# A mixture-of-experts block on one core: logits and shared first product merged, shared second products on two row tiles, later loads behind the first weights

## The chip, the cores and the metric

The kernel runs on one core of one Trainium2 chip. The time is the device time of one execution in microseconds; less is better.

## The reference

The input has 8 samples of 512 tokens of 128 numbers, all float32. Three sublayers follow each other, each on a layer norm of the running value x: a mixture-of-experts block (added at half weight), a gated mixing block, and the same mixture-of-experts block again with the same weights.

```python
# the experts, on xf of 512 tokens x 128 per sample
shared = silu(xf @ Ws_up) @ Ws_down                 # 128 -> 64 -> 128
aff = xf @ centroids.T                              # logits of 64 experts
idx = top_k(aff + expert_biases, 8)
w = sigmoid(aff[idx]); w = w / (sum(w) + 1e-8)      # cw: weights, 0 elsewhere
h = silu(einsum('td,edf->etf', xf, W_up))           # all 64 experts, 128 -> 64
y = einsum('etf,efd->etd', h, W_down)               # 64 -> 128
out = shared + einsum('etd,te->td', y, cw)

# the mixing block
xf = concat([u[:, :1], u[:, 1:] @ WB.T]);  xb = concat([u[:, 1:] @ WBf.T, u[:, -1:]])
gamma = sigmoid(xf @ w1.T + xb @ w2.T + b)
y = gamma * (xf + xb) + (1 - gamma) * u
```

In xf the first token of a sample is taken over unmultiplied, in xb the last one.

## The kernel before

The work is cut into 16 items: sample s in layer 0 for s = 0 to 7, then the same samples in layer 1. An item has its 512 tokens in the free dimension. `ut` is its normed input turned to [128 numbers, 512 tokens].

Two experts make a pair, so that a pair's hidden rows fill 128 partitions; an item has 32 pairs. With the shared expert as block 0 it has 33 blocks, and one loop over n = 0, 1, ... runs through the blocks of all items. In step n the order of the work is written out by hand:

- `up(n)`, L376: one product of the pair's first weights with `ut` into `ph` (four PSUM buffers), and a Silu on ScalarE into `h` (L385, L387). For block 0 the weights are `wsup`, with 64 columns.
- `scale(n - 16)`, L390: VectorE multiplies `h` by the experts' weights `cw`, which lie on the 64 partitions of each expert (L397). Block 0 is not scaled. A group of `cw` holds four pairs, and four such buffers exist; when a group is used up, `load_cw` (L288) issues the load of the group four further on, as two transfers of 512 KB that spread a row to 64 partitions.
- `down(n - 19)`, L403: one product of `h` with the pair's second weights, summed in `y` over the 33 blocks (L410). For block 0 the weights are `wsdn`, with 64 rows. After an item's last block ScalarE halves `y` into `yt`, and two steps later `finish` (L360) turns it back into `po` and VectorE adds it to x.
- one slice of `prep(i + 1)`, L301, a generator that prepares the next item and starts in its predecessor's block 1 (for the first item in block `SCALE_LAG - 2` = 14): for layer 1 first `mix`; then the norm, the turn into `ut` (L313), the logits `pa` (four products with 64 columns, L318), the choice of eight experts on VectorE with a Sigmoid on ScalarE (L327, with a change of function table there and back), and the turn of the weights into `pc` (four transposes, L353), copied to `cw_sb` and written to `cw_t` in HBM (L357), from where `load_cw` spreads them.

In `mix`, the two results of a tile of tokens are summed in PSUM as `pfb` by a product with `mix_b` (L236) and one with `mix_bf` (L244); for the first and last tile a third product with the matrices `first` and `last` (L233, L252) puts in the token that is not multiplied. `make_mix` prepares the mix weights, in slices during item 1.

All loads are issued on one queue, SP, in the order of the program: x of sample 0, `cent`, `wsup`, the first weights `wup` in four transfers (one eighth, one eighth, one quarter and one half of them), `wsdn`, the second weights `wdn` in four transfers with x of sample 1 between, the other samples (L97), and the mix weights (L137 to L144). What `prep` and `load_cw` issue for the first item stands behind all these on the queue.

Of the kernel before, what the change touches and what calls it, by code (L numbers as in the profile page):

```python
# [8 lines left out]
F32 = mybir.dt.float32  # L9
AF = mybir.ActivationFunctionType  # L10
ALU = mybir.AluOpType
AX = mybir.AxisListType

P = 128
# [1 line left out]
EPS_W = 1e-8  # L16
LOWEST = -3.4028234663852886e38
GROUP = 4
SCALE_LAG = 16
DOWN_LAG = 19  # L20
CW_BUFS = 4


@with_exitstack
def macaron_kernel(
# [27 lines left out]

    nc = tc.nc
    B, T, D = x.shape
    E, _, F = w_up.shape
    NT = T // P
    NP = E // 2  # L60
    NG = NP // GROUP
    D1 = D + 1
    assert D == P and 2 * F == P and NP % GROUP == 0

    const = ctx.enter_context(tc.tile_pool(name="const", bufs=1))
    resid = ctx.enter_context(tc.tile_pool(name="resid", bufs=1))
# [16 lines left out]
    make_identity(nc, ident)  # L83
    minus_half = const.tile([P, NT], F32, name="minus_half")
    nc.gpsimd.memset(minus_half, -0.5)

    first = const.tile([P, P], F32, name="first")
    last = const.tile([P, P], F32, name="last")
    nc.gpsimd.memset(first, 0.0)
    nc.gpsimd.memset(last, 0.0)  # L90
    nc.gpsimd.tensor_copy(first[:, 0:1], ident[:, 0:1])
    nc.gpsimd.tensor_copy(last[:, P - 1 : P], ident[:, P - 1 : P])
    warm = const.tile([P, 1], F32, name="warm")
    nc.scalar.activation(warm, ident[:, 0:1], AF.Silu)

    def load_x(s):
        nc.sync.dma_start(out=xs[s], in_=x[s].rearrange("(n p) d -> p n d", p=P))  # L97

    wup = const.tile([P, E, F], F32, name="wup")
    wdn = const.tile([P, NP, D], F32, name="wdn")  # L100
    wsup = const.tile([P, F], F32, name="wsup")
    wsdn = const.tile([F, D], F32, name="wsdn")
    cent = const.tile([E, D], F32, name="cent")
    bias_bc = const.tile([P, E], F32, name="bias_bc")
    wb_sb = const.tile([D, D], F32, name="wb_sb")
# [10 lines left out]
    def load_down(e0, e1):  # L116
        nc.sync.dma_start(  # L117
            out=wdn[:, e0 // 2 : e1 // 2, :],
            in_=w_down[e0:e1].rearrange("(q two) f d -> (two f) q d", two=2),
        )  # L120

    load_x(0)
    nc.sync.dma_start(out=cent, in_=centroids)
    nc.sync.dma_start(out=wsup, in_=ws_up)
    load_up(0, E // 8)
    nc.sync.dma_start(out=bias_bc, in_=expert_biases.partition_broadcast(P))
    load_up(E // 8, E // 4)
    load_up(E // 4, E // 2)
    load_up(E // 2, E)
    nc.sync.dma_start(out=wsdn, in_=ws_down)  # L130
    load_down(0, E // 4)
    load_x(1)
    for e0 in range(E // 4, E, E // 4):
        load_down(e0, e0 + E // 4)
    for s in range(2, B):
        load_x(s)
    nc.sync.dma_start(out=wb_sb, in_=wb)  # L137
    nc.sync.dma_start(out=wbf_sb, in_=wbf)
    nc.sync.dma_start(out=w12[:, 0, :], in_=w1[0].partition_broadcast(P))
    nc.sync.dma_start(out=w12[:, 1, :], in_=w2[0].partition_broadcast(P))  # L140
    with nc.allow_non_contiguous_dma(reason="two columns, once"):
        nc.sync.dma_start(out=w12c[:, 0:1], in_=w1.rearrange("o d -> d o"))
        nc.sync.dma_start(out=w12c[:, 1:2], in_=w2.rearrange("o d -> d o"))
    nc.sync.dma_start(out=b_bc, in_=b.partition_broadcast(P))  # L144

    def transposed(dst, src, rows):
        ps = ps_m.tile([P, 512], F32, tag="m", name="turn_ps")
        nc.tensor.transpose(ps[:, :rows], src, ident[:rows, :rows])
        nc.scalar.copy(dst, ps[:, :rows])

    cent_t = const.tile([P, E], F32, name="cent_t")
    transposed(cent_t, cent, E)

    mix_b = const.tile([P, D1], F32, name="mix_b")
    mix_bf = const.tile([P, D1], F32, name="mix_bf")
# [47 lines left out]
    def mix(s):  # L203
# [22 lines left out]
        for half in range(NT // 2):  # L226
            pfb = ps_m.tile([P, 2, D1], F32, tag="m", name=f"pfb{s}_{half}")
            halves.append(pfb)
            for k in range(2):
                j = 2 * half + k  # L230
                edge = j == 0
                if edge:
                    nc.tensor.matmul(  # L233
                        pfb[:, k, :], lhsT=first, rhs=u[:, j, :], start=True, stop=False
                    )
                nc.tensor.matmul(  # L236
                    pfb[:, k, :],
                    lhsT=ut[:, j * P : (j + 1) * P],
                    rhs=mix_b,
                    start=not edge,  # L240
                    stop=False,
                )
                edge = j == NT - 1
                nc.tensor.matmul(  # L244
                    pfb[:, k, :],
                    lhsT=ut[:, j * P + 1 : (j + 1) * P + 1],
                    rhs=mix_bf,
                    start=False,
                    stop=not edge,
                )  # L250
                if edge:
                    nc.tensor.matmul(  # L252
                        pfb[:, k, :], lhsT=last, rhs=u[:, j, :], start=False, stop=True
                    )
            nc.scalar.activation(  # L255
                gam[:, 2 * half : 2 * half + 2],
                pfb[:, :, D],
                AF.Tanh,
                bias=half_b,
                scale=0.5,  # L260
            )
            yield
# [19 lines left out]

    items = [(layer, s) for layer in range(2) for s in range(B)]
    uts = {}
    cw_ts = {}
    cw_tiles = {}

# [13 lines left out]
    def prep(i):  # L301

        layer, s = items[i]
# [9 lines left out]
        nc.scalar.copy(ut, ps)  # L313
        uts[i] = ut
        yield
        pa = ps_m.tile([P, NT, E], F32, tag="m", name=f"pa{i}")
        for j in range(NT):
            nc.tensor.matmul(  # L318
                pa[:, j, :], lhsT=ut[:, j * P : (j + 1) * P], rhs=cent_t, start=True, stop=True
            )  # L320
        yield
        biased = route.tile([P, NT, E], F32, tag="biased", name=f"biased{i}")
# [25 lines left out]
        )  # L348
        yield
        yield  # L350
        pc = ps_m.tile([P, 512], F32, tag="m", name=f"pc{i}")
        for j in range(NT):
            nc.tensor.transpose(pc[:E, j * P : (j + 1) * P], cw[:, j, :], ident)  # L353
        cw_sb = route.tile([E, T], F32, tag="cw_sb", name=f"cw_sb{i}")
        nc.scalar.copy(cw_sb, pc[:E, :])  # L355
        cw_t = dram.tile([E, T], F32, tag="cw_t", name=f"cw_t{i}")
        nc.sync.dma_start(out=cw_t, in_=cw_sb)  # L357
        cw_ts[i] = cw_t

    def finish(i, yt):  # L360
# [7 lines left out]
            nc.sync.dma_start(out=out[s].rearrange("(n p) d -> p n d", p=P), in_=xs[s])  # L368


    NB = NP + 1
    hs = {}
    ys = {}
    later = {}

    def up(n):  # L376
        i, blk = divmod(n, NB)
        rows = F if blk == 0 else P
        ph = ps_up.tile([P, T], F32, tag="ph", name=f"ph{n}")
        if blk == 0:  # L380
            w = wsup
        else:
            pair = blk - 1
            w = wup[:, 2 * pair : 2 * pair + 2, :].rearrange("d e f -> d (e f)")
        nc.tensor.matmul(ph[:rows, :], lhsT=w, rhs=uts[i], start=True, stop=True)  # L385
        h = hid.tile([P, T], F32, tag="h", name=f"h{n}")
        nc.scalar.activation(h[:rows, :], ph[:rows, :], AF.Silu)  # L387
        hs[n] = h

    def scale(n):  # L390
        i, blk = divmod(n, NB)
        if blk == 0:
            return
        q, g = divmod(blk - 1, GROUP)
        group = i * NG + q
        h = hs[n]
        nc.vector.tensor_tensor(h, h, cw_tiles[group][:, g, :], ALU.mult)  # L397
        if g == GROUP - 1:
            cw_tiles.pop(group)
            if group + CW_BUFS < len(items) * NG:  # L400
                load_cw(group + CW_BUFS)

    def down(n):  # L403
        i, blk = divmod(n, NB)
        if blk == 0:
            ys[i] = ps_y.tile([P, T], F32, tag="y", name=f"y{i}")
            w, h = wsdn, hs.pop(n)[:F, :]
        else:
            w, h = wdn[:, blk - 1, :], hs.pop(n)
        nc.tensor.matmul(ys[i], lhsT=w, rhs=h, start=blk == 0, stop=blk == NB - 1)  # L410
        if blk == NB - 1:
            yt = norm.tile([P, T], F32, tag="yt", name=f"yt{i}")
            nc.scalar.mul(yt, ys.pop(i), 0.5)  # L413
            later[n + 2] = lambda: finish(i, yt)

    total = len(items) * NB
    coming = prep(0)
    while 0 not in uts:
        next(coming)
    mixing = make_mix()  # L420
    for n in range(total + DOWN_LAG):
        i, blk = divmod(n, NB)
        if n < total:
            if blk == 0 and i > 0:
                for _ in coming or ():
                    pass
            if i > 0 and blk == 1 or i == 0 and blk == SCALE_LAG - 2:
                for _ in coming or ():
                    pass
                if i == 0:  # L430
                    for g in range(CW_BUFS):
                        load_cw(g)
                coming = prep(i + 1) if i + 1 < len(items) else None
            up(n)
        if 0 <= n - SCALE_LAG < total:
            scale(n - SCALE_LAG)
        if n >= DOWN_LAG:
            down(n - DOWN_LAG)
        if n - DOWN_LAG in later:
            later.pop(n - DOWN_LAG)()  # L440
        if coming is not None and n < total:
            next(coming, None)
        if i == 1 and n < total:
            next(mixing, None)
    for k in sorted(later):
        later[k]()
# [40 lines left out]
```

## Time and profile before

| what | value |
|---|---|
| median of 3 runs | 1003.58 us (1003.48 to 1003.65) |
| profiled execution, its own time | 1002.36 us |
| span of the profiled execution | 1000.6 us |
| mean granted clock of TensorE | 0.996 |
| TensorE busy | 982.5 us, 98% of the span |
| VectorE, ScalarE, GpSimd busy | 457.8, 399.7, 40.0 us |
| HBM traffic | 145 GB/s over the span |

TensorE is written PE, VectorE DVE, ScalarE ACT, GpSimd POOL, the load queue SP or SPq. A float32 product appears as two records, one for each of two passes, and a float32 transpose as one. Matmuls are pipelined and the ends of their records are modelled, so records of neighbours overlap: what a product costs is read from the distance between starts.

### The profile page before, as it was taken

What the parts mean: (1) busy time and instruction counts of PE and PEld (TensorE: products, weight loads), DVE (VectorE), ACT (ScalarE), POOL (GpSimd) and SP (SyncE); (2) the same over time, 40 slices, a digit from 0 to 9 for tenths busy, and PEclk for the clock granted to TensorE, in tenths of its full rate; (3) what the DMA queues carried; (4) which work ended last, traced back from release to release, by engine and by line L of the source; (5) the groups of instructions that cost most, each with busy time, mean ns of one, the idle gap of its engine ahead of it and who ended that gap; (6) DMA issues with size and microseconds to landing.
All of it is one profiled execution on the core that took longest, in us unless ns stands there. A gap on an engine that the chain in (4) does not pass through costs nothing.

```text
span 1000.6 us, 8408 instructions
## 1 busy us (share of the span) xinstructions
PE 982.5 (98%) x2631; PEld 451.6 (45%) x2631; DVE 457.8 (46%) x1232; ACT 399.7 (40%) x656; POOL 40.0 (4%) x75
## 2 busy tenths in 40 slices
PE   7799999999999999999999999999999999999997
PEld 3344444444444444454444544445444454444443
DVE  3344544234453324636256362563626637166051
ACT  4434343443434334334343343433434334343330
POOL 1000000000000000000000000000000000000000
PEclk9899999999999999999999999999999999999999
DMA  9899757578665678737749377593775937659751
GB/s 230 181 215 202 145 113 148 117 163 169 142 140 119 145 138 174 162 85 156 150 106 193 83 168 144 112 201 84 167 142 117 203 80 170 134 120 206 153 125 23
DMA packets 90206, 145.67 MB, mean 146 GB/s; under 512 B 9648, under 2 KB 23600, under 8 KB 90160
## 3 DMA queue, kind: packets, MB, share of 16 engines
q1 hardware_dynamic: 90160, 145.12, 69.4%
q8 instruction: 21, 0.34, 0.2%
q14 instruction: 25, 0.20, 0.1%
HBM read 140.90 MB, written 4.19 MB: 145 GB/s over the span
## 4 chain that ended last, share of the span: by engine, by line
PE 95%; SPq 2%; DMA 2%; DVE 0%; issue 0%; ACT 0%; DVEq 0%
PE y L410 46%; PE ph L385 44%; PE pa L318 1%; PE po L365 1%; PE pfb L244 1%; PE pfb L236 1%; DMA cw<-cw_t 1%; PE pc L353 1%; SPq L97 1%; PE ps_ft L200 1%; DMA x<-in_L_attn_u_dram 1%; SPq L112 0%; SPq L117 0%; SPq L130 0%; DMA cw_t<-cw_sb 0%; PE ps_mixt L200 0%
## 5 line engine op out<-in xcount | busy, mean ns | idle before, releaser
L410 PE MATMUL y<-h,wdn 128*128 128x512 f32 x1024 | 522.4, 595 | 6.0 <-DVE h L397 6.0
L385 PE MATMUL ph<-ut,wup 128*128 128x512 f32 x1024 | 525.9, 598 | 0.0
L387 ACT ACTIVATE h<-ph 128x512 f32<-128x512 f32 (+1 forms) x528 | 313.2, 597 | 508.1 <-PE ph L385 475.7
L397 DVE TENSOR_TENSOR h<-h,cw 128x512 f32<-128x512 f32 x512 | 319.0, 682 | 40.4 <-DMA cw<-cw_t 35.0
L410 PEld LDWEIGHTS y<-h,wdn 128*128 128x128 f32 x1024 | 193.5, 190 | 256.5 <-issue 214.1
L385 PEld LDWEIGHTS ph<-ut,wup 128*128 128x128 f32 x1024 | 188.1, 191 | 213.0 <-issue 201.1
L366 DVE TENSOR_TENSOR x<-po,x 128x512 f32<-128x512 f32 x16 | 11.1, 692 | 171.2 <-PE po L365 171.2
L264 DVE TENSOR_SCALAR sg<-gam 128x4 f32<-128x4 f32 x8 | 1.4, 170 | 162.1 <-ACT gam L255 162.1
L323 DVE TENSOR_TENSOR biased<-pa,bias_bc 128x256 f32<-128x256 f32 x16 | 6.8, 424 | 122.0 <-PE pa L318 122.0
L179 POOL TENSOR_SCALAR rstd_f<-mv_f 128x4 f32<-128x4 f32 x16 | 8.5, 532 | 585.8 <-DVE mv_f L177 585.8
L186 DVE TENSOR_SCALAR u_f<-x,mv_f,rstd_f 128x128 f32<-128x128 f32 x64 | 17.8, 342 | 20.4 <-POOL rstd_f L180 20.4
L318 PEld LDWEIGHTS pa<-cent_t,ut 128*128 128x128 f32 x128 | 17.5, 200 | 9.0 <-issue 8.3
L327 ACT ACT_TABLE_LOAD x16 | 20.5, 1283 | 0.3
L387 ACT ACT_TABLE_LOAD x16 | 20.5, 1283 | 0.3
L385 PE MATMUL ph<-ut,wsup 128*64 128x512 f32 x32 | 18.1, 647 | 0.7 <-ACT ut L313 0.7
L410 PE MATMUL y<-h,wsdn 64*128 64x512 f32 x32 | 18.0, 641 | 0.0
L413 ACT ACTIVATE yt<-y 128x512 f32<-128x512 f32 x16 | 9.6, 597 | 20.5 <-PE y L410 20.5
L318 PE MATMUL pa<-cent_t,ut 128*128 128x64 f32 x128 | 17.1, 279 | 0.0
L180 POOL TENSOR_TENSOR rstd_f<-rstd_f,minus_half 128x4 f32<-128x4 f32 x16 | 16.6, 1038 | 1.3
L175 DVE BATCH_NORM_STATS2 st_f<-x 128x6 f32<-128x128 f32 x64 | 13.8, 276 | 3.5 <-DMA x<-in_L_attn_u_dram 3.5
L355 ACT COPY cw_sb<-pc 64x512 f32<-64x512 f32 x16 | 9.3, 580 | 14.0 <-PE pc L353 12.9
L179 POOL TENSOR_SCALAR rstd_mix<-mv_mix 128x4 f32<-128x4 f32 x8 | 4.6, 577 | 253.6 <-DVE mv_mix L177 253.6
(72 smaller groups left out, 280.0 us busy)
## 6 DMA issues: line engine op xcount, KB each, us to landing
cw<-cw_t SPq DMA_DIRECT2D x256, 512.0 KB, 8.2
x<-in_L_attn_u_dram SPq DMA_DIRECT2D x8, 256.0 KB, 5.5
wdn<-in_L_ffn_W_down_dram SPq DMA_DIRECT2D x4, 512.0 KB, 6.5
cw_t<-cw_sb SPq DMA_DIRECT2D x16, 128.0 KB, 3.3
out_dram<-x SPq DMA_DIRECT2D x8, 256.0 KB, 2.8
wup<-in_L_ffn_W_up_dram SPq DMA_DIRECT2D x2, 256.0 KB, 3.7
wup<-in_L_ffn_W_up_dram SPq DMA_DIRECT2D x1, 512.0 KB, 6.2
w<-in_L_attn_w_dram SPq DMA_DIRECT2D x2, 64.0 KB, 4.8
```

Of the source, the lines that this page charges most:

```text
L97: nc.sync.dma_start(out=xs[s], in_=x[s].rearrange("(n p) d -> p n d", p=P))
L175: nc.vector.bn_stats(st[:, j, :], src[:, j, :])
L179: nc.gpsimd.tensor_scalar(rstd, mv[:, :, 1], EPS_LN, None, ALU.add)
L180: nc.gpsimd.tensor_tensor(rstd, rstd, minus_half, ALU.pow)
L186: nc.vector.tensor_scalar(u[:, j, :D], src[:, j, :], mv[:, j, 0:1], rstd[:, j : j + 1], ALU.subtract, ALU.mult,)
L318: nc.tensor.matmul(pa[:, j, :], lhsT=ut[:, j * P : (j + 1) * P], rhs=cent_t, start=True, stop=True)
L327: nc.scalar.activation(sig, pa, AF.Sigmoid)
L366: nc.vector.tensor_tensor(xs[s], po, xs[s], ALU.add)
L385: nc.tensor.matmul(ph[:rows, :], lhsT=w, rhs=uts[i], start=True, stop=True)
L387: nc.scalar.activation(h[:rows, :], ph[:rows, :], AF.Silu)
L397: nc.vector.tensor_tensor(h, h, cw_tiles[group][:, g, :], ALU.mult)
L410: nc.tensor.matmul(ys[i], lhsT=w, rhs=h, start=blk == 0, stop=blk == NB - 1)
```

## The change

- One tile `wsl` [128, 2, 2, 64] holds the logits' and the shared expert's first weights twice, in both orders. For each half of the tokens one product `sl` of 128 columns gives both: for the first half the shared rows on partitions 0 to 63 and the logits on 64 to 127, for the second half the other way round. VectorE copies the logits to `lg`, ScalarE applies Silu to the shared rows into `hsh`, both [128, 256]: the two halves of the tokens on the two halves of the partitions. Block 0 is gone; an item has 32 steps.
- The logits are turned by two 128 x 128 transposes into `pa`. The weights `cw` are turned by two transposes into `pc` [128, 256], in place of four, and written by two transfers.
- The shared second product is made for half of the tokens at a time with 64 rows of `wsdn`, which lies on both halves of the partitions. During an even item i, after the downs of pairs 8 and 16, two such products follow each other: one for item i on one half of the partitions, one for item i + 1 on the other, each into its own item's `y`.
- In `mix` the products with `first` and `last` are gone; VectorE adds the token to `pfb` ahead of tanh. The two matrices and their four GpSimd operations go.
- On the SP queue x of sample 1 stands ahead of `wdn`, of which half follows in two transfers; the rest (`wsdn` twice, the other half of `wdn`, the samples from 2 on, the mix weights) is issued after the first four groups of `cw`.
- `SCALE_LAG` is 22 and `DOWN_LAG` 25; `h` has 28 buffers for 22. `prep(1)` starts in pair 14 of item 0, and `make_mix` runs during item 2.

The diff, cut:

```diff
-SCALE_LAG = 16
-DOWN_LAG = 19
+SCALE_LAG = 22
+DOWN_LAG = 25
 CW_BUFS = 4
+FIRST = 14
+SHARED = (8, 16)
...
-    wsup = const.tile([P, F], F32, name="wsup")
-    wsdn = const.tile([F, D], F32, name="wsdn")
+    wsl = const.tile([P, 2, 2, F], F32, name="wsl")
+    wsdn = const.tile([P, D], F32, name="wsdn")
...
-    nc.sync.dma_start(out=wsup, in_=ws_up)
+    for k in range(2):
+        nc.sync.dma_start(out=wsl[:, k, k, :], in_=ws_up)
     load_up(0, E // 8)
...
-    nc.sync.dma_start(out=wsdn, in_=ws_down)
+    load_x(1)
     load_down(0, E // 4)
-    load_x(1)
-    for e0 in range(E // 4, E, E // 4):
-        load_down(e0, e0 + E // 4)
...
+    load_down(E // 4, E // 2)
+
+    def load_rest():
+        for k in range(2):
+            nc.sync.dma_start(out=wsdn[k * F : (k + 1) * F, :], in_=ws_down)
+        load_down(E // 2, E)
+        for s in range(2, B):
+            load_x(s)
+        nc.sync.dma_start(out=wb_sb, in_=wb)
...
+    for k in range(2):
+        nc.scalar.copy(wsl[:, k, 1 - k, :], turn_ps[:, :E])
...
-                if edge:
-                    nc.tensor.matmul(
-                        pfb[:, k, :], lhsT=last, rhs=u[:, j, :], start=False, stop=True
-                    )
+            k, j, at = ((0, 0, 0), (1, NT - 1, P - 1))[half]
+            nc.vector.scalar_tensor_tensor(
+                pfb[:, k, :], u[:, j, :], ident[:, at : at + 1], pfb[:, k, :], ALU.mult, ALU.add
+            )
...
+        for k in range(2):
+            nc.tensor.matmul(
+                sl[:, k, :],
+                lhsT=wsl[:, k, :, :].rearrange("d a f -> d (a f)"),
+                rhs=ut[:, k * H : (k + 1) * H],
+                start=True,
+                stop=True,
+            )
+            at, other = slice(k * F, (k + 1) * F), slice((1 - k) * F, (2 - k) * F)
+            nc.vector.tensor_copy(lg[other, :], sl[other, k, :])
+            nc.scalar.activation(hsh[at, :], sl[at, k, :], AF.Silu)
+        shared[i] = hsh
+        yield
         pa = ps_m.tile([P, NT, E], F32, tag="m", name=f"pa{i}")
-        for j in range(NT):
-            nc.tensor.matmul(
-                pa[:, j, :], lhsT=ut[:, j * P : (j + 1) * P], rhs=cent_t, start=True, stop=True
+        for j in range(NH):
+            nc.tensor.transpose(
+                pa[:, 2 * j : 2 * j + 2, :].rearrange("p c e -> p (c e)"),
+                lg[:, j * P : (j + 1) * P],
+                ident,
             )
...
-        for j in range(NT):
-            nc.tensor.transpose(pc[:E, j * P : (j + 1) * P], cw[:, j, :], ident)
...
+        for j in range(NH):
+            nc.tensor.transpose(
+                pc[:, j * P : (j + 1) * P],
+                cw[:, 2 * j : 2 * j + 2, :].rearrange("p c e -> p (c e)"),
+                ident,
+            )
...
-        nc.sync.dma_start(out=cw_t, in_=cw_sb)
+        nc.sync.dma_start(out=cw_t[:, H:], in_=cw_sb[:E, :])
+        nc.sync.dma_start(out=cw_t[:, :H], in_=cw_sb[E:, :])
...
+        if i % 2 == 0 and pair in SHARED:
+            if i + 1 not in ys:
+                ys[i + 1] = ps_y.tile([P, T], F32, tag="y", name=f"y{i + 1}")
+            k = SHARED.index(pair)
+            for at, item in sorted(((k, i), (1 - k, i + 1))):
+                rows = slice(at * F, (at + 1) * F)
+                nc.tensor.matmul(
+                    ys[item][:, at * H : (at + 1) * H],
+                    lhsT=wsdn[rows, :],
+                    rhs=shared[item][rows, :],
+                    start=item > i and k == 0,
+                    stop=False,
+                )
...
                 if i == 0:
                     for g in range(CW_BUFS):
                         load_cw(g)
+                    load_rest()
```

More of the change, by code (lines that the diff above doesn't have):

```diff
@@ L62, in macaron_kernel @@
     D1 = D + 1
-    assert D == P and 2 * F == P and NP % GROUP == 0
+    H = T // 2
+    NH = NT // 2
+    assert D == P and 2 * F == P and E == F and NT == 4 and NP % GROUP == 0
     const = ctx.enter_context(tc.tile_pool(name="const", bufs=1))
@@ L85, in macaron_kernel @@
     nc.gpsimd.memset(minus_half, -0.5)
[L87 to L92, printed above, removed]
     warm = const.tile([P, 1], F32, name="warm")
@@ L129, in macaron_kernel @@
     load_up(E // 2, E)
-    nc.sync.dma_start(out=wsdn, in_=ws_down)
+    load_x(1)
     load_down(0, E // 4)
-    load_x(1)
-    for e0 in range(E // 4, E, E // 4):
-        load_down(e0, e0 + E // 4)
[L135 to L144, printed above, removed]
+    load_down(E // 4, E // 2)
[6 more added lines that the diff above has]
+        nc.sync.dma_start(out=wb_sb, in_=wb)
+        nc.sync.dma_start(out=wbf_sb, in_=wbf)
+        nc.sync.dma_start(out=w12[:, 0, :], in_=w1[0].partition_broadcast(P))
+        nc.sync.dma_start(out=w12[:, 1, :], in_=w2[0].partition_broadcast(P))
+        with nc.allow_non_contiguous_dma(reason="two columns, once"):
+            nc.sync.dma_start(out=w12c[:, 0:1], in_=w1.rearrange("o d -> d o"))
+            nc.sync.dma_start(out=w12c[:, 1:2], in_=w2.rearrange("o d -> d o"))
+        nc.sync.dma_start(out=b_bc, in_=b.partition_broadcast(P))
     def transposed(dst, src, rows):
@@ L149, in transposed @@
         nc.scalar.copy(dst, ps[:, :rows])
-    cent_t = const.tile([P, E], F32, name="cent_t")
-    transposed(cent_t, cent, E)
+    turn_ps = ps_m.tile([P, 512], F32, tag="m", name="cent_ps")
+    nc.tensor.transpose(turn_ps[:, :E], cent, ident[:E, :E])
+    for k in range(2):
+        nc.scalar.copy(wsl[:, k, 1 - k, :], turn_ps[:, :E])
     mix_b = const.tile([P, D1], F32, name="mix_b")
@@ L230, in mix @@
                 j = 2 * half + k
-                edge = j == 0
-                if edge:
-                    nc.tensor.matmul(
-                        pfb[:, k, :], lhsT=first, rhs=u[:, j, :], start=True, stop=False
-                    )
                 nc.tensor.matmul(
@@ L239, in mix @@
                     rhs=mix_b,
-                    start=not edge,
+                    start=True,
                     stop=False,
                 )
-                edge = j == NT - 1
                 nc.tensor.matmul(
@@ L248, in mix @@
                     start=False,
-                    stop=not edge,
+                    stop=True,
                 )
-                if edge:
-                    nc.tensor.matmul(
-                        pfb[:, k, :], lhsT=last, rhs=u[:, j, :], start=False, stop=True
-                    )
+            k, j, at = ((0, 0, 0), (1, NT - 1, P - 1))[half]
+            nc.vector.scalar_tensor_tensor(
+                pfb[:, k, :], u[:, j, :], ident[:, at : at + 1], pfb[:, k, :], ALU.mult, ALU.add
+            )
             nc.scalar.activation(
@@ L284, in macaron_kernel @@
     uts = {}
+    shared = {}
     cw_ts = {}
@@ L315, in prep @@
         yield
-        pa = ps_m.tile([P, NT, E], F32, tag="m", name=f"pa{i}")
-        for j in range(NT):
-            nc.tensor.matmul(
-                pa[:, j, :], lhsT=ut[:, j * P : (j + 1) * P], rhs=cent_t, start=True, stop=True
+        sl = ps_m.tile([P, 2, H], F32, tag="m", name=f"sl{i}")
+        hsh = small.tile([P, H], F32, tag="hsh", name=f"hsh{i}")
+        lg = route.tile([P, H], F32, tag="lg", name=f"lg{i}")
+        for k in range(2):
[3 more added lines that the diff above has]
+                rhs=ut[:, k * H : (k + 1) * H],
+                start=True,
+                stop=True,
+            )
[4 more added lines that the diff above has]
+        yield
+        pa = ps_m.tile([P, NT, E], F32, tag="m", name=f"pa{i}")
+        for j in range(NH):
[3 more added lines that the diff above has]
+                ident,
             )
@@ L350, in prep @@
         yield
-        pc = ps_m.tile([P, 512], F32, tag="m", name=f"pc{i}")
-        for j in range(NT):
-            nc.tensor.transpose(pc[:E, j * P : (j + 1) * P], cw[:, j, :], ident)
-        cw_sb = route.tile([E, T], F32, tag="cw_sb", name=f"cw_sb{i}")
-        nc.scalar.copy(cw_sb, pc[:E, :])
+        pc = ps_m.tile([P, H], F32, tag="m", name=f"pc{i}")
+        for j in range(NH):
[4 more added lines that the diff above has]
+            )
+        cw_sb = route.tile([P, H], F32, tag="cw_sb", name=f"cw_sb{i}")
+        nc.scalar.copy(cw_sb, pc)
         cw_t = dram.tile([E, T], F32, tag="cw_t", name=f"cw_t{i}")
-        nc.sync.dma_start(out=cw_t, in_=cw_sb)
+        nc.sync.dma_start(out=cw_t[:, H:], in_=cw_sb[:E, :])
+        nc.sync.dma_start(out=cw_t[:, :H], in_=cw_sb[E:, :])
         cw_ts[i] = cw_t
@@ L368, in finish @@
             nc.sync.dma_start(out=out[s].rearrange("(n p) d -> p n d", p=P), in_=xs[s])
-    NB = NP + 1
     hs = {}
@@ L376, in up @@
     def up(n):
-        i, blk = divmod(n, NB)
-        rows = F if blk == 0 else P
+        i, pair = divmod(n, NP)
         ph = ps_up.tile([P, T], F32, tag="ph", name=f"ph{n}")
[L380 to L385, printed above, removed]
+        w = wup[:, 2 * pair : 2 * pair + 2, :].rearrange("d e f -> d (e f)")
+        nc.tensor.matmul(ph, lhsT=w, rhs=uts[i], start=True, stop=True)
         h = hid.tile([P, T], F32, tag="h", name=f"h{n}")
-        nc.scalar.activation(h[:rows, :], ph[:rows, :], AF.Silu)
+        nc.scalar.activation(h, ph, AF.Silu)
         hs[n] = h
     def scale(n):
[L391 to L395, printed above, removed]
+        group, g = divmod(n, GROUP)
         h = hs[n]
@@ L403, in down @@
     def down(n):
-        i, blk = divmod(n, NB)
-        if blk == 0:
+        i, pair = divmod(n, NP)
+        if pair == 0 and i not in ys:
             ys[i] = ps_y.tile([P, T], F32, tag="y", name=f"y{i}")
[L407 to L411, printed above, removed]
+        nc.tensor.matmul(
+            ys[i],
+            lhsT=wdn[:, pair, :],
+            rhs=hs.pop(n),
+            start=pair == 0 and i % 2 == 0,
+            stop=pair == NP - 1,
+        )
[5 more added lines that the diff above has]
+                rows = slice(at * F, (at + 1) * F)
+                nc.tensor.matmul(
+                    ys[item][:, at * H : (at + 1) * H],
[3 more added lines that the diff above has]
+                    stop=False,
+                )
+        if pair == NP - 1:
             yt = norm.tile([P, T], F32, tag="yt", name=f"yt{i}")
@@ L414, in down @@
             later[n + 2] = lambda: finish(i, yt)
-    total = len(items) * NB
+    total = len(items) * NP
     coming = prep(0)
-    while 0 not in uts:
+    while 0 not in shared:
         next(coming)
@@ L421, in macaron_kernel @@
     for n in range(total + DOWN_LAG):
-        i, blk = divmod(n, NB)
+        i, pair = divmod(n, NP)
         if n < total:
-            if blk == 0 and i > 0:
+            if pair == 0 and i > 0:
                 for _ in coming or ():
                     pass
-            if i > 0 and blk == 1 or i == 0 and blk == SCALE_LAG - 2:
+            if i > 0 and pair == 1 or i == 0 and pair == FIRST:
                 for _ in coming or ():
@@ L442, in macaron_kernel @@
             next(coming, None)
-        if i == 1 and n < total:
+        if i == 2 and n < total:
             next(mixing, None)
```

## The prediction

> **What bounds the kernel now.** I read the head of the page and its chain first, then TensorE's groups by form, then TensorE's timeline around each odd matmul, then the start with all engines. From the page:
>
> ```profile
> span 1000.6 us, 8408 instructions
> ...
> PE 982.5 (98%) x2631; PEld 451.6 (45%) x2631; DVE 457.8 (46%) x1232; ACT 399.7 (40%) x656; POOL 40.0 (4%) x75
> ...
> PE 95%; SPq 2%; DMA 2%; DVE 0%; issue 0%; ACT 0%; DVEq 0%
> ```
>
> TensorE holds 95% of the chain and no other engine is half busy. What leaves TensorE shortens the run; what moves among the others does not, unless it makes TensorE wait. The groups by form (the columns are busy, mean ns of one record; a product has two) give the candidates:
>
> ```profile
> L385 PE MATMUL ph<-ut,wsup 128*64 128x512 f32 x32 | 18.1, 647 | 0.7 <-ACT ut L313 0.7
> L410 PE MATMUL y<-h,wsdn 64*128 64x512 f32 x32 | 18.0, 641 | 0.0
> L318 PE MATMUL pa<-cent_t,ut 128*128 128x64 f32 x128 | 17.1, 279 | 0.0
> L353 PE MATMUL pc<-ident,cwtok 128*64 128x128 f32 x64 | 9.6, 273 | 0.0
> L252 PE MATMUL pfb<-u_mix,last 128*128 128x129 f32 x16 | 3.1, 274 | 0.0
> ```
>
> These means include pipeline time that overlaps the next record, so I price by distance between starts. TensorE's timeline (start, length, operation):
>
> ```profile
> 302.29 1.02 PE L410 MATMUL y<-h,wdn 128*128 128x512 f32 x2
> 303.24 1.07 PE L385 MATMUL ph<-ut,wsup 128*64 128x512 f32 x2
> 304.24 1.12 PE L410 MATMUL y<-h,wdn 128*128 128x512 f32 x2
> 305.20 1.02 PE L385 MATMUL ph<-ut,wup 128*128 128x512 f32 x2
> ...
> 337.88 1.02 PE L385 MATMUL ph<-ut,wup 128*128 128x512 f32 x2
> 338.83 1.12 PE L410 MATMUL y<-h,wsdn 64*128 64x512 f32 x2
> 339.88 1.12 PE L385 MATMUL ph<-ut,wup 128*128 128x512 f32 x2
> 340.84 1.02 PE L410 MATMUL y<-h,wdn 128*128 128x512 f32 x2
> ```
>
> Ordinary products start 0.859 us apart (two passes of 0.43). Three products around wsup take 2.91 us, so wsup costs 2.91 - 2 x 0.859 = 1.19; wsdn likewise 2.96 - 1.72 = 1.24. A half-array product thus costs 0.33 to 0.38 more than a full one. The same subtraction at 313.37 to 315.98 prices the four logits products at 0.89 (eight passes of 0.107). The four pc transposes take 0.44, 0.11 each, as do the 128 x 128 ones of ps_ft and po. Products of 129 columns stand 0.22 apart.
>
> The start, all engines (start, length, queue or engine):
>
> ```profile
> 20.20 0.59 ACT L355 COPY cw_sb<-pc 64x512 f32<-64x512 f32 x1
> ...
> 28.51 0.49 SPq L357 DMA_DIRECT2D cw_t<-cw_sb  x1
> ...
> 32.15 18.67 SPq L296 DMA_DIRECT2D cw<-cw_t  x12
> ...
> 39.95 1.90 DVE L397 TENSOR_TENSOR h<-h,cw 128x512 f32<-128x512 f32 x3 [18.02 <-DMA cw<-cw_t]
> 40.69 2.07 PE L410 MATMUL y<-h,wdn 128*128 128x512 f32 x2 [5.95 <-DVE h L397]
> ```
>
> The first weights cw are ready at 20.8 but written at 28.5, since SP first issues every load down to b_bc (27.6). That ends in TensorE's only long wait, 5.95. It costs more: the granted clock is 0.68 from 41 to 45 us, and down, up to the next down take 3.22 instead of 1.72. So 6.1 (34.6, where that down would have started, to 40.69) + 1.5 = 7.6 us.
>
> **What the Trainium skill says.** "TensorEngine Tiling (Array Packing)", Key Properties: changing the tiling mode drains TensorE, changing the tile does not. The trace agrees on the first: a bubble of about 0.2 into wsdn's mode and 0.19 out. No trace of before shows the second. "TensorE: Matmul & The Clock Gate", Part 3: products on different row groups run side by side, but start and end in program order; four tiles gained 3.07 there. Not shown before. Same page, HAM oscillation: idle gaps above about 3.4 us halve the clock; the stall above agrees. "PSUM — Partial Sum Buffer", bank collisions: two row tiles must not write one bank together. Here the two products of a group go to the y of two items, two banks.
>
> **The change, part by part** (16 items).
>
> Removed per item: wsup 1.19, wsdn 1.24, logits 0.89, pc 0.44: 3.77.
>
> Added per item: the product sl, 2 x 256 columns on the full array, no mode change. A pass should take half of 0.43 plus little, 0.216, longer than the 0.107 a weight load needs (the logits' rate). Four passes: 0.87. Then two pa and two pc transposes at 0.11: 0.44.
>
> The shared second products: one group of two 64-row, 256-column products per item on average. Bubbles 0.39 in all, plus four passes of 0.216. If the second product overlaps only the first one's second pass (order kept), three slots: 0.65 + 0.39 = **1.04**, my value. Bounds: wholly side by side 0.43 + 0.39 = 0.82; one after the other 1.25; that with another bubble between, 1.45.
>
> Sum per item: 0.87 + 0.44 + 1.04 - 3.77 = -1.42, times 16 = **-22.7** (-26.2 to -16.2).
>
> Mix: L233 and L252 go, two products of 0.22 in each of 8 items: **-3.5**. In their place VectorE gets two scalar_tensor_tensor (0.34 each, as L268) ahead of tanh. VectorE is 46% busy and downs trail scales by three steps of 1.72, 5.2 us: no cost unless VectorE is already that late. Dropping first and last takes four operations from POOL, idle there anyway.
>
> New work elsewhere: per item two VectorE copies lg (0.42 at most, as biased, also 128x256) and two Silus of 64x256 (about 0.38, as rsig) for one of 0.59; the cw_sb copy halves to about 0.38. They hide beside TensorE. One wait is new: pa now needs lg from VectorE, where before it needed only ut from ScalarE. Between sl and pa stand one up and one down, 1.72 us, against about 0.2 + 2 x 0.42: 0.7 spare. Each hsh Silu waits for its lg copy, and the ups' Silus queue behind; four ph buffers (6.9 us) cover that in the steady state.
>
> SP: one more wsup load (0.57) moves the first up load from 2.45 to 3.0; it lands within about 4 us, before its product at 10. The cw_t write becomes two issues per item, SP being mostly free later.
>
> The start: cw_sb is ready at about 20.5 and the SP queue is empty, so the writes issue at 20.5 and 21, land about 3.4 later, and cw loads begin at 24.5. The first group lands 7.8 later (as 32.15 to 39.95), at 32.3. TensorE reaches the first scale (step 22) at 35 and the first down (step 25) near 38. The stall goes: **-7.6**.
>
> What is late next there: ScalarE. Around steps 18 to 21 it has four Silus, ut, two hsh, sigmoid and two table loads of 1.28, about 7.0 us, while TensorE issues only ups, 0.86 apart, into four buffers. By my walk the Silu of up 21 ends at 37.9, and up 25, which needs its buffer, would start at 36.9: **+1.1** (0 to 2). The table loads fell into the long stall before.
>
> The loads moved behind cw (wsdn twice, half of wdn, x2 to x7, mix weights, 2.9 MB) stand on SP ahead of group 4. Four groups are 4.2 MB, which land at about 215 GB/s (the rate from 36 us on), done at 46; the moved loads at 290 (the rate of 16.5 to 25 us) end near 56; group 4 lands near 63. Its scale is due at step 38, 61.7, its down at 67. VectorE waits, TensorE does not. x2 lands near 51, its statistics are due at 52.
>
> The longer lags move downs from the loop to the tail, each 0.86 in either place: no cost. Scales there need 0.68 against 0.86.
>
> Against wall price, the cold clock until about 16.5 lets slightly less through at the start: +0.2.
>
> Sum: -22.7 - 3.5 - 7.6 + 1.1 + 0.2 = **-32.5**. Against the profiled execution's own 1002.36 (span 1000.6 and 1.8 around it): 969.9. The median shown is 1.2 above that execution: 1003.6 - 32.5 = **971.1 us**.
>
> **The rivals.**
> A. The row tiles don't overlap: +0.21 to +0.41 per item, 974.5 to 977.7. For it: wsdn's 0.38 of bubbles; the passes of one product come first. Against: the page's rule on tiles. Chance 0.22. The opposite, wholly side by side: 967.6, 0.1.
> B. The start's stall moves. If group 4 lands after 67, TensorE waits again; 5 us and 1.5 of cold clock give 977.6. For: SP is in order, 2.9 MB stand ahead. Against: 4 us spare. Chance 0.13.
> C. Slower: pa's new wait on lg. VectorE works in order; a scale waiting for cw (35.0 us in 10 waits in before, 11.7 in 6 between 45 and 965) delays lg, and TensorE, with pa next in order, stalls with no three-step lag. It needs over 32.5 / 16 = 2.0 us at each item, so VectorE 2.7 late every time; at 2.5 a stall the time is 1011. Before's longest wait in that stretch is 3.0, but few. Chance 0.03.
> D. The operations don't leave TensorE (a compiled sl or transpose costs what it replaces): within 2 us of before, 0.01.
> The forecast, 968 to 974, has the remaining 0.51.
>
> **How the numbers follow.** About 0.2%, 2 us, is what the measurement can tell from no change. All cases but C and D are faster: 0.96; same 0.01; slower 0.03. The range 963.5 to 980 takes in the side-by-side case, A and B; A with B (about 984) and C lie outside.
>
> **What would show it.** After: PE busy near 955 of a span near 968; sl passes 0.22 apart; pa and pc two records each of 0.11; from the down before a shared group to the down after it about 1.04 more than without it; no wait of y on h at 35 to 41, a wait of ph on ScalarE's h of about 1 us there; cw_t issued near 20.5. I am wrong on tiles if the groups cost 1.25 or more, on the start if SP or cw still carries a wait of several us, and altogether if TensorE shows waits in every item.

## The result, and the profile after

The changed kernel takes 985.5 us (four runs, 985.12 to 985.68) against 1003.5: a ratio of 0.982 (95% interval 0.9803 to 0.9837). It is shorter by 18.0 us or 1.8%, far outside the spread of the runs, where 32.5 us were forecast; it lies 14.4 above the forecast and 5.5 above the range. The profiled execution took 985.12 us (span 983.0).

Head and chain of the page of the changed kernel:

```profile
span 983.0 us, 8249 instructions
...
PE 954.5 (97%) x2535; PEld 440.8 (45%) x2535; DVE 476.2 (48%) x1280; ACT 398.8 (41%) x673; POOL 39.5 (4%) x71
...
PE 96%; ACT 1%; DVE 1%; DMA 0%; issue 0%; POOL 0%; ACTq 0%
```

TensorE's busy time is 954.5, as forecast (955); the span is not (983 for 968). That the busy time fits is partly luck: the records of sl take 22.0 us here and 17.6 in the first experiment, where the new waits are gone and the busy time is 950.8. Time appeared in which TensorE stands still: 28.5 us outside its busy time, where before had 18.1. The waits of TensorE show for what (line, what it waited for: us in total, times, longest):

```profile
PE sl L327 <- ACT hsh L336: 14.9, 16, 0.9
PE cent_ps L159 <- DMA cent<-in_L_ffn_centroids_dram: 4.0, 1, 4.0
PE ps_ft L209 <- DVE u_f L195: 2.4, 1, 2.4
PE ph L410 <- ACT h L412: 1.7, 2, 0.9
```

Sixteen waits, one per item, each of the same length: a wait built into the code, not a late transfer. The prediction had named waits in every item as the sign that it is wrong altogether. The wait of y on h of before (6.0) is gone, and the one of ph on ScalarE that was expected in its place is there, 0.86 long at 39.98 us. A second one of 0.86 stands at 19.48, in the first item, where none was forecast. TensorE's groups by form (busy, mean ns of one record, idle time before them and what ended it):

```profile
L327 PE MATMUL sl<-ut,wsl 128*128 128x256 f32 x64 | 22.0, 426 | 15.5 <-ACT hsh L336 14.9 <-ACT ut L318 0.7
...
L443 PE MATMUL y<-hsh,wsdn 64*128 64x256 f32 x64 | 11.2, 428 | 0.0
...
L342 PE MATMUL pa<-ident,lg 128*128 128x128 f32 x32 | 6.4, 282 | 0.0
L379 PE MATMUL pc<-ident,cwtok 128*128 128x128 f32 x32 | 6.1, 273 | 0.0
```

One item in the timeline of the changed kernel (start, length, engine, operation, idle time before it and its releaser):

```profile
620.35 1.02 PE L428 MATMUL y<-h,wdn 128*128 128x512 f32 x2
...
621.20 0.59 PE L327 MATMUL sl<-ut,wsl 128*128 128x256 f32 x2
621.84 0.43 DVE L335 COPY lg<-sl 64x256 f32<-64x256 f32 x1 [2.60 <-PE sl L327]
622.30 0.38 ACT L336 ACTIVATE hsh<-sl 64x256 f32<-64x256 f32 x1 [1.16 <-DVE lg L335]
622.73 0.70 PE L327 MATMUL sl<-ut,wsl 128*128 128x256 f32 x2 [0.93 <-ACT hsh L336]
623.26 1.02 PE L410 MATMUL ph<-ut,wup 128*128 128x512 f32 x2
...
624.12 1.02 PE L428 MATMUL y<-h,wdn 128*128 128x512 f32 x2
624.98 0.38 PE L342 MATMUL pa<-ident,lg 128*128 128x128 f32 x2
```

The two products sl start 1.53 us apart, not 0.43. Between them stand VectorE's copy of the first half and then ScalarE's Silu of it. The program issues product, copy, Silu, product, copy, Silu, and both products write one tile of PSUM, the memory that takes TensorE's results: the second product waits until the first half has been read, although it writes the other half. From the down at 620.35 to the one at 624.12 are 3.77 us; less an up and a down (1.72), sl costs 2.05 in place of 0.87. Further down pa follows without a wait, 0.22 for its two transposes.

A shared group in the timeline:

```profile
655.90 1.02 PE L428 MATMUL y<-h,wdn 128*128 128x512 f32 x2
656.85 0.70 PE L443 MATMUL y<-hsh,wsdn 64*128 64x256 f32 x4
657.49 1.12 PE L410 MATMUL ph<-ut,wup 128*128 128x512 f32 x2
658.45 1.02 PE L428 MATMUL y<-h,wdn 128*128 128x512 f32 x2
```

From down to down are 2.55 us, so the group costs 2.55 - 1.72 = 0.83: four passes of 0.216 fit into the time of two, plus the bubbles of about 0.2 on each side.

The start:

```profile
21.67 0.52 SPq L387 DMA_DIRECT2D cw_t<-cw_sb  x1
...
36.62 0.68 DVE L418 TENSOR_TENSOR h<-h,cw 128x512 f32<-128x512 f32 x1
...
39.98 1.13 PE L410 MATMUL ph<-ut,wup 128*128 128x512 f32 x2 [0.86 <-ACT h L412]
...
40.95 1.02 PE L428 MATMUL y<-h,wdn 128*128 128x512 f32 x2
```

The first weights are written at 21.7 for 28.5, the first scale runs at 36.6, and the first down follows its up without a wait on it. The clock is 1.00 from 33 to 45 us.

### The profile page after: what moved, and what is told of

Its sections match the earlier page's. It is cut to its first block, busy times and chain, and to the rows that moved or that the text cites. A ratio compares the mean times of both kernels' runs of the same rounds, so it can differ in the third digit from the quotient of the medians.

```text
span 983.0 us, 8249 instructions
## 1 busy us (share of the span) xinstructions
PE 954.5 (97%) x2535; PEld 440.8 (45%) x2535; DVE 476.2 (48%) x1280; ACT 398.8 (41%) x673; POOL 39.5 (4%) x71
## 4 chain that ended last, share of the span: by engine, by line
PE 96%; ACT 1%; DVE 1%; DMA 0%; issue 0%; POOL 0%; ACTq 0%
PE y L428 45%; PE ph L410 44%; PE sl L327 2%; PE y L443 1%; PE ps_ft L209 1%; PE po L396 1%; PE pfb L247 1%; PE pfb L240 1%; DVE lg L335 1%; ACT hsh L336 1%; PE pa L342 0%; PE pc L379 0%; PE ps_mixt L209 0%; DMA x<-in_L_attn_u_dram 0%; ACT L412 0%
## 5 line engine op out<-in xcount | busy, mean ns | idle before, releaser
L412 ACT ACTIVATE h<-ph 128x512 f32<-128x512 f32 x512 | 303.4, 597 | 456.8 <-PE ph L410 429.4
L335 DVE COPY lg<-sl 64x256 f32<-64x256 f32 x32 | 13.5, 422 | 108.8 <-PE sl L327 108.8
L256 DVE SCALAR_TENSOR_TENSOR pfb<-u_mix,ident,pfb 128x129 f32<-128x129 f32 x16 | 5.7, 356 | 93.8 <-PE pfb L247 80.1
L327 PE MATMUL sl<-ut,wsl 128*128 128x256 f32 x64 | 22.0, 426 | 15.5 <-ACT hsh L336 14.9
L336 ACT ACTIVATE hsh<-sl 64x256 f32<-64x256 f32 x32 | 12.1, 378 | 38.7 <-DVE lg L335 38.7
L327 PEld LDWEIGHTS sl<-ut,wsl 128*128 128x128 f32 x64 | 11.1, 196 | 30.0 <-ACT hsh L336 21.6
L318 ACT COPY ut<-ps_ft 128x512 f32<-128x512 f32 x16 | 9.4, 586 | 14.1 <-PE ps_ft L209 14.1
L259 ACT ACTIVATE gam<-pfb,half_b 128x2 f32<-128x2 f32 x16 | 4.2, 262 | 25.2 <-DVE pfb L256 25.2
```

What stands on the lines that cost most here:

```text
L327: nc.tensor.matmul(sl[:, k, :], lhsT=wsl[:, k, :, :].rearrange("d a f -> d (a f)"), rhs=ut[:, k * H : (k + 1) * H], start=True, stop=True,)
L335: nc.vector.tensor_copy(lg[other, :], sl[other, k, :])
L336: nc.scalar.activation(hsh[at, :], sl[at, k, :], AF.Silu)
L412: nc.scalar.activation(h, ph, AF.Silu)
```

## The experiments

Times are medians; the kernel before took 1003.72 us beside the first four and 1003.96 beside the last four. The first two experiments and the last one change only how the changed kernel makes sl. "Same rows", "short lags", "loads ahead" and "edge products" are built on the kernel with both products sl first and are compared with its 966.8 us; "only the loads" is built on the kernel before.

**Both products sl first.**

```diff
         for k in range(2):
             nc.tensor.matmul(
...
+        for k in range(2):
             at, other = slice(k * F, (k + 1) * F), slice((1 - k) * F, (2 - k) * F)
             nc.vector.tensor_copy(lg[other, :], sl[other, k, :])
             nc.scalar.activation(hsh[at, :], sl[at, k, :], AF.Silu)
```

> The changed kernel with both products sl issued ahead of the copies and Silus that read them; nothing else moves. Theory: the second product of each item waits for VectorE's copy and ScalarE's Silu of the first half because they share one PSUM tile, and that wait costs 2.06 - 0.87 = 1.19 us per item. Then TensorE shows no wait of sl on hsh, the two products start 0.43 apart, and the time is 985.5 - 16 x 1.19 = 966.4 us. Rival: the product of 128 x 128 by 256 columns is slow by itself (its weight loads are not hidden): then the order changes nothing, 985 us.

Measured: 966.8 us (ratio to before 0.9633, 0.962 to 0.9646). TensorE's waits no longer hold sl on hsh. In the timeline of this kernel an sl takes what it was priced at:

```profile
608.16 1.02 PE L429 MATMUL y<-h,wdn 128*128 128x512 f32 x2
...
609.02 1.03 PE L327 MATMUL sl<-ut,wsl 128*128 128x256 f32 x4
609.88 1.02 PE L411 MATMUL ph<-ut,wup 128*128 128x512 f32 x2
610.08 0.43 DVE L336 COPY lg<-sl 64x256 f32<-64x256 f32 x1 [3.03 <-PE sl L327]
610.54 0.38 ACT L337 ACTIVATE hsh<-sl 64x256 f32<-64x256 f32 x1 [1.59 <-DVE lg L336]
...
610.95 0.42 DVE L336 COPY lg<-sl 64x256 f32<-64x256 f32 x1 [0.44 <-ACT hsh L337]
...
611.60 0.38 PE L343 MATMUL pa<-ident,lg 128*128 128x128 f32 x2
```

Four passes in 0.86. The copies and Silus still take turns, but beside the next up and down. So pa gets its last logits at 611.37, only 0.23 before it starts; in item 1 it waits 0.6. The rival of a slow product falls.

**Two banks, order kept.**

```diff
-        sl = ps_m.tile([P, 2, H], F32, tag="m", name=f"sl{i}")
...
         for k in range(2):
+            sl = ps_m.tile([P, 1, H], F32, tag="m", name=f"sl{i}_{k}")
             nc.tensor.matmul(
-                sl[:, k, :],
+                sl[:, 0, :],
...
```

> The changed kernel with its order kept (product, copy, Silu, product, copy, Silu), but the two products write two PSUM tiles in two banks. If the wait comes from the shared tile and not from the order of the program, it goes here too: about 966 us, as with both products first. If the order is what holds the second product back, it stays at 985 us.

Measured: 966.34 us (0.9613 to 0.9639 of before), and no wait of sl on hsh. So neither the order of the program nor the shared tile costs by itself: the wait needs a reader between two writers of one tile, and either cure takes it away. The two tiles are also two banks, so this run does not tell whether the order is kept by tile or by bank.

```profile
547.50 1.03 PE L327 MATMUL sl<-ut,wsl 128*128 128x256 f32 x4
...
548.14 0.88 DVE L335 COPY lg<-sl 64x256 f32<-64x256 f32 x2 [3.42 <-PE sl L327]
...
548.60 0.83 ACT L336 ACTIVATE hsh<-sl 64x256 f32<-64x256 f32 x2 [1.15 <-DVE lg L335]
```

With two tiles the two copies follow each other without a gap, and the second runs beside the first Silu (548.60). With one tile they ran one after the other, though both only read, and on different partitions. The Silu thus lengthened the wait at sl: it came after the copy, not beside it.

**Same rows for both products of a group.**

```diff
-                rows = slice(at * F, (at + 1) * F)
+                rows = slice(0, F)
```

> As with both products sl first, but the two shared second products of a group use the same 64 rows (0 to 63) of wsdn and hsh, so half of the shared second products read the wrong half of the tokens; counts and shapes are the same. If the two row tiles run wholly side by side, as the 0.83 us that a group costs in the changed kernel says, losing this costs two passes of 0.216 in each of 16 groups: 6.9 us above the kernel with both products first, about 973.3. If the 0.83 has another cause, the time stays near 966.4.

Measured: 973.33 us, 6.5 above both products first. Timeline of this kernel around a group:

```profile
645.83 1.02 PE L429 MATMUL y<-h,wdn 128*128 128x512 f32 x2
646.78 1.13 PE L444 MATMUL y<-hsh,wsdn 64*128 64x256 f32 x4
647.84 1.12 PE L411 MATMUL ph<-ut,wup 128*128 128x512 f32 x2
648.80 1.02 PE L429 MATMUL y<-h,wdn 128*128 128x512 f32 x2
```

Now 2.97 from down to down, so 1.25 a group: the same work one after the other costs 0.42 more, just two passes. The row tiles (the two halves of the rows, one for each product) do run side by side, wholly. In the kernel with both products first, the window from 643.40 to 643.48 us, at the start of a group (643.47), shows how (two records, length in ns, start):

```profile
L444 PE MATMUL y<-hsh,wsdn x2: 480/480/480, 643.5 to 643.5; 64*128 64x256 f32 x2
```

Two of the four passes start together, where the prediction let the first one start alone.

**Only the loads reordered, in the kernel before.**

```diff
+    load_x(1)
     load_down(0, E // 4)
...
+    load_down(E // 4, E // 2)
+
+    def load_rest():
+        load_down(E // 2, E)
+        for s in range(2, B):
+            load_x(s)
...
                     for g in range(CW_BUFS):
                         load_cw(g)
+                    load_rest()
...
-        if i == 1 and n < total:
+        if i == 2 and n < total:
```

> The kernel before with only its loads reordered: x of sample 1 ahead, half of wdn, the other samples and the mix weights behind the first four groups of cw, mix weights prepared in item 2; lags 16 and 19 and all products as before. Theory: the first cw_t is written near 21 in place of 28.5, the stall of 5.95 and the 1.5 us of slow clock go: 1003.5 - 7 = 996.5 us. Rival: it is the longer lags that remove the stall; then part of it stays, 1000 to 1003 us.

Measured: 998.32 us (0.9938 to 0.9963 of before): 5.4 faster, not 7. The first down runs at 34.6 without a wait, so the first theory holds at that place. But its timeline shows another wait later:

```profile
64.65 1.29 DVE L399 TENSOR_TENSOR h<-h,cw 128x512 f32<-128x512 f32 x2 [15.98 <-DMA cw<-cw_t]
65.40 1.18 PE L412 MATMUL y<-h,wdn 128*128 128x512 f32 x2 [2.42 <-DVE h L399]
66.38 1.91 PE L387 MATMUL ph<-ut,wup 128*128 128x512 f32 x2
68.08 1.86 PE L412 MATMUL y<-h,wdn 128*128 128x512 f32 x2
```

The same by stretch (from and to, length, busy of TensorE, weight load, VectorE, ScalarE and GpSimd with their counts, granted clock, DMA share, GB/s):

```profile
60.00:66.00 6.00, 3.58 (x9) 1.32 (x9) 1.35 (x3) 1.38 (x3) 0.00 (x0) 1.00 1.07 213
66.00:70.00 4.00, 4.00 (x9) 1.54 (x8) 2.75 (x14) 0.60 (x1) 1.61 (x2) 0.57 1.06 235
```

This is the prediction's rival B in the flesh: the fifth group of cw stands behind the moved loads and TensorE waits 2.42 us, then runs its products 1.70 apart (66.38 to 68.08), at half speed. The wait itself takes back 2.4 of the 7.6 us that the start had cost. The profiled execution is the slowest of the five; their mean clocks are 0.997, 0.999, 0.999, 0.997 and 0.999, and such a half-speed stretch takes about 0.002 off the mean, so it probably came in two of five. With the old lags the stall is moved and made smaller, not removed.

**Short lags with the new loads.**

```diff
-SCALE_LAG = 22
-DOWN_LAG = 25
+SCALE_LAG = 16
+DOWN_LAG = 19
```

> The kernel with both products sl first, with the lags of before (16 and 19 in place of 22 and 25). Theory: the longer lags do not shorten the run by themselves, they give the moved loads room: with short lags the fifth group of cw (landing near 64.9 by the trace with both products first) is wanted by TensorE near 62.5, so TensorE waits 2 to 3 us once, with some slow clock after it: 968.5 to 971.5 us. Rival: the lags hide nothing more: 966.8 us.

Measured: 971.39 us, 4.6 above both products first, at the top of what was expected. TensorE's waits show y on h for 2.6 us and pa on lg for 1.3 (0.6 with long lags); the clock is 0.59 from 66 to 70 us.

**Loads ahead of cw again, lags kept long.**

```diff
+    load_rest()
+
     def transposed(dst, src, rows):
...
                         load_cw(g)
-                    load_rest()
```

> The kernel with both products sl first, with the loads issued all ahead of the first cw as before (wsdn, the second half of wdn, the other samples, mix weights); lags 22 and 25. Theory: cw_t is written near 28.5 again and the first group of cw lands near 40, while TensorE wants the first down at 39.5: it waits 1 to 2.5 us, too short to slow the clock: 968 to 969.5 us. So the longer lags alone take most of the stall and the order of loads the rest. Rival: the order of loads is what takes the stall: it comes back with 5 us or more, above 971.5.

Measured: 973.34 us, 6.5 above both products first. Theory and rival were told apart by 971.5, so the rival has the time. The theory was right on the wait, though: the first down starts at 41.6 after 2.17 us. It was wrong on the clock. TensorE's timeline and the busy times by stretch, columns as above:

```profile
38.33 1.12 PE L413 MATMUL ph<-ut,wup 128*128 128x512 f32 x2 [0.86 <-ACT h L415]
41.62 2.08 PE L431 MATMUL y<-h,wdn 128*128 128x512 f32 x2 [2.17 <-DVE h L421]
44.38 0.66 PE L382 MATMUL pc<-ident,cwtok 128*128 128x128 f32 x2 [0.69 <-DVE cwtok L375]
```

```profile
36.00:41.00 5.00, 2.59 (x6) 0.68 (x4) 0.12 (x1) 4.20 (x7) 0.00 (x0) 0.95 1.06 212
41.00:45.00 4.00, 2.69 (x5) 1.15 (x6) 3.79 (x10) 0.00 (x0) 0.00 (x0) 0.50 1.06 205
45.00:49.00 4.00, 4.00 (x8) 1.61 (x7) 2.94 (x5) 1.10 (x3) 0.00 (x0) 0.71 1.07 210
```

No wait is over 2.2 us, and yet the clock is 0.50 from 41 to 45. The mean of 0.95 from 36 to 41 puts the fall to 0.50 at about 40.5: in the second wait, some 1 us after that began, and before the third (0.69), which ran at half clock already. So the order of loads and the lags need each other: either alone leaves 4.6 to 6.5 us on the table.

**The edge products put back.**

```diff
+                edge = j == 0
+                if edge:
+                    nc.tensor.matmul(
+                        pfb[:, k, :], lhsT=first, rhs=u[:, j, :], start=True, stop=False
+                    )
...
-            nc.vector.scalar_tensor_tensor(
-                pfb[:, k, :], u[:, j, :], ident[:, at : at + 1], pfb[:, k, :], ALU.mult, ALU.add
-            )
...
+                    nc.tensor.matmul(
+                        pfb[:, k, :], lhsT=last, rhs=u[:, j, :], start=False, stop=True
+                    )
```

> The kernel with both products sl first, with the products with the matrices first and last put back into mix in place of the two VectorE operations. Theory: 16 products of 0.22 us return to TensorE and nothing else changes: 966.8 + 3.5 = 970.3 us. If VectorE's two operations ahead of tanh cost something in the changed kernel, the time rises by less than 3.5.

Measured: 970.24 us, 3.4 above both products first, so the two VectorE operations cost nothing that shows.

**Two banks and both products first.**

```diff
-        sl = ps_m.tile([P, 2, H], F32, tag="m", name=f"sl{i}")
...
+        sls = []
         for k in range(2):
+            sl = ps_m.tile([P, 1, H], F32, tag="m", name=f"sl{i}_{k}")
+            sls.append(sl)
             nc.tensor.matmul(
...
+        for k in range(2):
             at, other = slice(k * F, (k + 1) * F), slice((1 - k) * F, (2 - k) * F)
-            nc.vector.tensor_copy(lg[other, :], sl[other, k, :])
-            nc.scalar.activation(hsh[at, :], sl[at, k, :], AF.Silu)
+            nc.vector.tensor_copy(lg[other, :], sls[k][other, 0, :])
+            nc.scalar.activation(hsh[at, :], sls[k][at, 0, :], AF.Silu)
```

> Both products sl first and into two PSUM tiles. Theory: nothing is left to gain in the steady state; only the single wait of 0.6 us of pa for lg in item 1 can go: 966.2 to 966.8 us. If the sharing of one bank by the copies and the Silus still held TensorE back somewhere, it would be lower.

Measured: 966.0 us (0.9609 to 0.9635 of before), the lowest median, but not told apart from the two simpler cures: its runs (965.65 to 966.13) overlap those with two banks (964.8 to 966.4). The single wait of pa on lg (0.6 us in item 1) is gone from TensorE's waits, as it is with two banks alone.

## Why the prediction was wrong

**The step that failed** is "Added per item: the product sl", with "Four passes: 0.87", and the sentence "One wait is new: pa now needs lg". The passes were priced right (0.86 with both products first). But two waits are new. The second is at the product itself. I followed the copies to whoever needs them next and not back to the tile they read: the second product writes it too, so it queues behind copy and Silu of the first half, and with it all of TensorE. That costs 2.05 - 0.86 = 1.19 us per item, 19.0 in 16 items; taking it away gave 985.5 - 966.8 = 18.7. A wait sat in the loop body, hidden by nothing, since TensorE is the engine that sets the time.

**The shared groups** were mis-sized the other way: 0.83 measured, 1.04 taken. The assumption that the second product overlaps only the first one's second pass was wrong; the bound "wholly side by side", given a chance of 0.1, holds. 16 x 0.21 = 3.4 us better.

**Right**: pa and pc at 0.11 a transpose; mix, -3.5 forecast and 3.4 measured; the start's stall gone, an early cw_t, and a wait of ph on ScalarE in its place (0.86 for 1.1; the other 0.86, in the first item, was missed). The walk behind that 1.1 put ScalarE's operations at about 7.0 us; their durations as listed add up to 6.7. **Rival B** did not come, thanks to the longer lags; with short ones it does. I had called the longer lags free and given them no gain of their own. They were worth 4.6 us here.

**Rival C** named the right trouble in the wrong place: a per-item wait of TensorE in order, on VectorE's handling of sl. pa had enough room (0.22 without a wait); the second sl had none. The 0.7 us to spare that I gave pa held by chance, as the late second sl pushes pa back too: I had counted two copies and left out that the Silu takes its turn between them. With both products first the room is 0.23.

The sum with measured terms: removed 3.77, added 2.05 + 0.44 + 0.83 = 3.32, so -0.45 per item, -7.2 in all; mix -3.4; the rest, -7.4, is the start (-6.3 forecast; this term is a remainder and not measured alone). Together -18.0. Without the wait at sl the kernel takes 966.8, 4.3 under the forecast of 971.1: 3.4 from the groups, and about 1 that fits the start's remainder.

## What to carry to other kernels

When an edit splits a result into parts of one PSUM tile, list who writes and who reads that tile in issue order: a reader placed between two writers makes the second writer wait for it, even when it writes another part, and if the writer is the bounding engine the wait is paid each time. Issue all writers first, or give each part its own tile. Moving loads later and lengthening a software pipeline's lag belong together: the first decides which data come late, the second whether the bounding engine notices.

## What was not expected of the hardware

Float32 products of 64 rows on two row tiles overlap fully though each has two passes and their order in the program is one product after the other: 0.83 a group against 1.25 on the same rows. Going from one row tile to the other costs nothing that shows, while going into and out of the 64-row mode leaves 0.40 beside the two passes of 0.216, near the 0.39 of bubbles that the prediction read from before.

TensorE's clock fell without a long wait. With only the loads reordered, a wait of 2.42 us was followed by a clock of 0.57 from 66 to 70 us in the profiled execution, and the fall came after 66, when TensorE had been running again since 65.40. With the loads ahead, it fell at about 40.5, in a wait of 2.17 that followed one of 0.86. The page "TensorE: Matmul & The Clock Gate" of the Trainium skill, section on HAM oscillation, sets the mark at gaps above about 3.4 us; here shorter ones were enough, and the measurement decides. The stall of before, which the prediction called in agreement, does not test the mark:

```profile
33.00:41.00 8.00, 2.05 (x5) 0.61 (x4) 1.05 (x2) 1.55 (x2) 0.00 (x0) 0.73 0.89 196
```

A mean clock of 0.73 over these 8 us puts a fall to 0.50 at about 36.7, when the wait begun at 34.7 was 2 us old. What exactly the clock follows is not shown here. The 0.9 us waits at every sl, one in some 60 us, left the clock at 0.999.
